# Twelve matmuls without a reader behind the last product of layer 0's MLP, ahead of layer 1's first keys

## The chip, the cores and the metric

The kernel runs on one core of one Trainium2 chip. The metric is the device time of one execution in microseconds (us); the number compared is the median of several executions. TensorE is called PE in the profile, its weight loads PEld, VectorE DVE, ScalarE ACT, GpSimd POOL, and SyncE, which here only issues DMAs, SP.

## The reference

Four layers run one after another on four images of 192 channels and 64 x 64 pixels, all in float32. Layer 0 is a deformable attention block that ends with an MLP; layer 1 is a full attention over the 4096 pixels of an image; layer 2 is attention in overlapping windows with a gated MLP; layer 3 is a depthwise convolution with computed weights. The change lies where layer 0 ends and layer 1 begins:

```python
# layer 0, its end
h1 = layer_norm(xs2, gamma2, beta2)
m = gelu(h1 @ w_fc1 + b_fc1) @ w_fc2 + b_fc2          # 192 -> 768 -> 192
x = xs2 + m
# layer 1
g_x = conv1x1(x, g_w, g_b);  theta_x = conv1x1(x, theta_w, theta_b);  phi_x = conv1x1(x, phi_w, phi_b)
f = softmax(einsum("bon,bom->bnm", theta_x, phi_x), axis=-1)          # 4096 x 4096
x = conv1x1(einsum("bnm,bom->bon", f, g_x), W_w, W_b) + x
```

## The kernel before, in words

The images are handled one by one, `b` from 0 to 3. For each image the stages follow each other so: layer 0's gather (its sampled pixels fetched by indirect DMAs into `ring`, L572, and weighted on ACT and DVE, L578 to L583), layer 0's MLP (`mlp0`), layer 1's keys and values (`keys`), layer 1's attention (`layer1`), layer 2's windows, and `rest`, which holds layer 2's MLP and layer 3. Work of the next image is laid beside that of the present one: the gather of image b+1 runs beside `layer1` of image b, and `mlp0` of image b+1 is a generator that `rest` of image b advances as it goes. Only image 0's `mlp0` runs alone. `offsets` of images 2 and 3, the convolution and the tables for the gather, is woven with `keys` of images 1 and 2. So beside `keys` of image 0 there are only the gather's first fetches, and beside `keys` of image 3 there is nothing.

The program is written through a tile framework. It places waits by the data that an instruction reads and writes, and it may order instructions of one engine otherwise than the text has them, by its own plan of times; within an engine the resulting order is fixed.

`mlp0` works on 8 chunks of 512 pixels (`NCH` is 8, `CN` is 512). The 192 channels are laid out as 128 rows and a second piece of 64. For a chunk, `widen` makes the 768 hidden channels (L796, L803) and applies Gelu on ACT (L809) into `gl`; `narrow(1)` (L821) and `narrow(0)` (L818) multiply by the second weight into a PSUM tile `p`, and one DVE instruction (L825) adds bias and input and writes the result over `x`. Then three DMAs on SP (L844) write the chunk to `x_flat`, in HBM.

`keys` reads the same image back, in 8 chunks of 512 pixels: a DMA on SP (L855) into a tile `xk` with two buffers, two products with `phiT` (L858, tile `tp`), an ACT copy with bias into `ph` (L859), eight small products with `gT` (L863, tile `g`), and a DVE copy into `gx` (L866). `layer1` then loads pieces `xc` of the image (L899), makes `th` from them (L902), and multiplies it with `ph` into scores `s` (L910).

`ident` (a 128 x 128 identity) and `bias` (layer 2's relative position bias, 128 rows of 384 numbers) are constants in SBUF that live from the first gather to the end.

One `nc.tensor.matmul` of float32 in the text appears as two MATMUL records in the trace: the two products at L858 of one chunk are four records.

## Time and profile before

| what | value |
|---|---|
| median of 3 runs | 6941.55 us (6940.37 to 6947.27) |
| the profiled execution's own time | 7023.62 us |
| its span | 7021.7 us |
| mean granted TensorE clock | 0.925 of full |
| PE busy | 6255.7 us, 89% of the span |
| DVE, ACT, POOL busy | 4813.5, 3724.2, 2070.0 us |
| PE's wait for `xk` at L858, by tile | 69.1 us with its weight loads, 11 times |

The profile comes from one execution with the profiler on. Its time is 82 us above the median of the others, so differences are made against its own span and carried over to the median. The views used are the page (busy times, the span in 40 slices, the costliest groups), the timeline (instructions in order, with the idle time before them and what ended it), busy time by stretches with the granted clock, one line's or one tile's instructions, and the chain of waits, which follows the work that ended last back in time. In the timeline a row is: start, duration of the merged group, engine, line, operation, output<-inputs, shape, count, and in brackets the idle time of the engine before it with what ended it.

### The profile page before, as it was taken

What the parts mean: (1) busy time and instruction counts of PE and PEld (TensorE: products, weight loads), DVE (VectorE), ACT (ScalarE), POOL (GpSimd) and SP (SyncE); (2) the same over time, 40 slices, a digit from 0 to 9 for tenths busy, and PEclk for the clock granted to TensorE, in tenths of its full rate; (3) what the DMA queues carried; (4) which work ended last, traced back from release to release, by engine and by line L of the source; (5) the groups of instructions that cost most, each with busy time, mean ns of one, the idle gap of its engine ahead of it and who ended that gap; (6) DMA issues with size and microseconds to landing.
All of it is one profiled execution on the core that took longest, in us unless ns stands there. A gap on an engine that the chain in (4) does not pass through costs nothing.

```text
span 7021.7 us, 114826 instructions
## 1 busy us (share of the span) xinstructions
PE 6255.7 (89%) x45020; PEld 4235.4 (60%) x45020; DVE 4813.5 (69%) x7087; ACT 3724.2 (53%) x6214; POOL 2070.0 (29%) x2265
## 2 busy tenths in 40 slices
PE   7677999998988899998988889999998889989976
PEld 3445578885643468886644458887554457766532
DVE  3654269984677759995586849996577757755656
ACT  3654368874544358884544348885444335535331
POOL 2654047761200037772200016773210000012100
PEclk8878989998999899998999999999999979989998
DMA  7885246761010177762010066773110010010000
GB/s 233 261 308 177 75 141 215 219 195 38 15 34 14 57 223 219 224 209 75 11 42 14 24 214 198 225 217 111 28 30 20 16 49 12 12 36 12 4 7 20
DMA packets 363195, 743.42 MB, mean 106 GB/s; under 512 B 52647, under 2 KB 246871, under 8 KB 361886
## 3 DMA queue, kind: packets, MB, share of 16 engines
q0 software_dynamic: 95040, 467.22, 20.9%
q1 hardware_dynamic: 267614, 268.87, 12.9%
q8 instruction: 355, 5.82, 0.4%
q14 instruction: 186, 1.52, 0.1%
HBM read 628.06 MB, written 106.21 MB: 105 GB/s over the span
## 4 chain that ended last, share of the span: by engine, by line
PE 65%; DVE 17%; ACT 7%; DMA 4%; issue 4%; another core or an unknown queue 1%; SPq 1%; POOL 1%; ACTq 0%; DVEq 0%; POOLq 0%
PE s L910 12%; PE y L976 11%; PE h L590 7%; PE v L1136 2%; PE qk L1061 2%; DVE ha L1304 2%; PE qk L1062 2%; PE h L1504 2%; DVE ga L1304 2%; PE po L482 1%; DMA ring<-table,idx 1%; PE t L1144 1%; DVE gate L1304 1%; PE zm L1515 1%; PE tp L858 1%
## 5 line engine op out<-in xcount | busy, mean ns | idle before, releaser
L572 POOL DMA_INDIRECT ring<-table,idx x1188 | 1677.8, 1412 | 1155.1 <-DVE row L579 281.1
L910 PE MATMUL s<-ths,ph 96*128 96x256 f32 x4096 | 985.6, 387 | 7.8 <-ACT ths L904 4.1
L910 PEld LDWEIGHTS s<-ths,ph 96*128 96x128 f32 x4096 | 788.3, 194 | 147.6 <-ACT ths L904 13.9
L578 ACT ACTIVATE row<-ring,pos 128x384 f32<-128x384 f32 x1188 | 697.6, 609 | 235.7 <-DVE xo L583 152.5
L579 DVE SCALAR_TENSOR_TENSOR row<-ring,fr,row 128x384 f32<-128x384 f32 x1188 | 698.9, 612 | 96.1 <-ACT row L578 73.2
L976 PE MATMUL y<-sc,gx 128*97 128x256 f32 x3008 | 723.5, 379 | 0.0
L582 ACT ACTIVATE xo<-row,pos 128x192 f32<-128x192 f32 x1188 | 505.7, 449 | 156.8 <-remote 60.4
L976 PEld LDWEIGHTS y<-sc,gx 128*97 128x97 f32 x3008 | 490.3, 164 | 122.4 <-issue 1.1
L583 DVE SCALAR_TENSOR_TENSOR xo<-row,fr,xo 128x192 f32<-128x192 f32 x1188 | 464.9, 411 | 117.4 <-ACT xo L582 64.8
L590 PE MATMUL h<-ti,xo 128*128 128x192 f32 x2376 | 465.1, 330 | 5.7 <-DVE xo L583 5.7
L912 ACT COPY sc<-s 128x1024 f32<-128x1024 f32 x376 | 377.0, 1003 | 170.6 <-PE s L910 162.2
L973 DVE TENSOR_TENSOR sc<-sc,mbs 128x1024 f32<-128x1024 f32 x376 | 448.6, 1217 | 15.0 <-ACT mbs L936 14.2
L917 DVE TENSOR_TENSOR top<-top,sc 128x1024 f32<-128x1024 f32 x282 | 344.3, 1221 | 130.8 <-ACT sc L912 119.9
L590 PEld LDWEIGHTS h<-ti,xo 128*128 128x128 f32 x2376 | 406.2, 191 | 42.6 <-DVE xo L583 10.7
L974 ACT ACTIVATE sc<-sc 128x1024 f32<-128x1024 f32 x376 | 393.2, 1054 | 27.7 <-DVE sc L973 19.2
L1120 DVE TENSOR_REDUCE es<-ex 128x6 f32<-128x384 f32 x264 | 133.2, 546 | 379.2 <-ACT ex L1116 379.2
L590 PE MATMUL h<-kept,xo 128*128 128x192 f32 x990 | 257.9, 396 | 120.5 <-DVE xo L583 59.7
L1545 POOL COPY gate<-gate 128x192 f32<-128x192 f32 x12 | 4.2, 348 | 1109.9 <-ACT gate L1538 1109.9
L590 PEld LDWEIGHTS h<-kept,xo 128*128 128x128 f32 x990 | 185.4, 221 | 207.7 <-DVE xo L583 95.9
L1304 DVE SCALAR_TENSOR_TENSOR ga<-gate,v,ga 128x1024 f32<-128x1024 f32 x234 | 299.7, 1281 | 7.2
L976 PE MATMUL y<-se,gx 128*97 128x256 f32 x1088 | 259.3, 379 | 0.5 <-ACT yn L982 0.5
L1509 ACT ACTIVATE z<-h,bias_fc1T 128x512 f32<-128x512 f32 x192 | 117.8, 686 | 232.8 <-PE h L1506 232.4
(383 smaller groups left out, 11530.6 us busy)
## 6 DMA issues: line engine op xcount, KB each, us to landing
ti<-table SPq DMA_DIRECT2D x396, 96.0 KB
table<-tt SPq DMA_DIRECT2D x24, 1056.0 KB
ring<-table,idx POOLq DMA_INDIRECT x1188
xnd<-xn SPq DMA_DIRECT2D x4, 3270.0 KB
table<-kept SPq DMA_DIRECT2D x12, 1056.0 KB
table<-tt SPq DMA_DIRECT2D x44, 288.0 KB
xi<-in_x_dram SPq DMA_DIRECT2D x32, 384.0 KB
xk<-xd SPq DMA_DIRECT2D x32, 384.0 KB
```

The lines of the kernel that those rows point to most:

```text
L572: nc.gpsimd.indirect_dma_start(out=gt.rearrange("p r q c -> p (r q c)"), out_offset=None, in_=table[:, :], in_offset=bass.IndirectOffsetOn ...
L578: nc.scalar.activation(row, gt[:, :, 0, :], AF.Copy, scale=pos[:, t, 9 + tap : 10 + tap])
L579: nc.vector.scalar_tensor_tensor(row, gt[:, :, 1, :], fr[:, t, 9 + tap : 10 + tap], row, ALU.mult, ALU.add)
L582: nc.scalar.activation(xo[:, j, :], row[:, 0, :], AF.Copy, scale=pos[:, t, tap : tap + 1])
L583: nc.vector.scalar_tensor_tensor(xo[:, j, :], row[:, 1, :], fr[:, t, tap : tap + 1], xo[:, j, :], ALU.mult, ALU.add)
L590: nc.tensor.matmul(acc[m // 2][:, bass.ts(m % 2, C)], lhsT=xo.rearrange("p j c -> p (j c)")[:, bass.ts(m, 128)], rhs=tt, start=t == 0 and ...
L910: nc.tensor.matmul(p[:, t, :], lhsT=ph[:, bass.ts(G * g + t, 128)], rhs=ths[i], start=True, stop=True)
L912: nc.scalar.copy(to, p)
L973: nc.vector.tensor_tensor(ex, ex, mbs[i].unsqueeze(1).to_broadcast([128, G, QN]), ALU.add)
L974: nc.scalar.activation(ex, ex, AF.Exp)
L976: nc.tensor.matmul(py, lhsT=gx[:, G * g + t, :], rhs=ex[:, t, :], start=g == 0 and t == 0, stop=g == NG - 1 and t == G - 1,)
L1304: nc.vector.scalar_tensor_tensor(acc[:, b], src(tap, b), w[:, tap : tap + 1], acc[:, b], ALU.mult, ALU.add)
```

## The change

Behind the last chunk's `narrow(0)` in `mlp0`, after the DMAs of its result were issued, `keep_warm` adds 12 products of `ident` with `bias`, each over 384 columns, into the PSUM tile `p` that `narrow(0)` returned. Each starts a new sum, and nothing reads `p` afterwards. `mlp0` is called once for each image, so 48 products are added in all. Nothing is taken away.

```diff
+    def keep_warm(p, n):
+
+        columns = bias.rearrange("p e h j -> p (e h j)")
+        for _ in range(n):
+            nc.tensor.matmul(p[:, 0:384], lhsT=ident, rhs=columns, start=True, stop=True)
+
     def mlp0(b, m2, pool, sb, ps):
...
                 nc.vector.scalar_tensor_tensor(to, p, VW["l0_bfc2"][:, k], to, ALU.add, ALU.add)
+                return p
...
             hn = norm(i + 1)
-            narrow(0)
+            p = narrow(0)
             for of, to in parts(x, HN, x_flat[b % 2], CN * i):
                 nc.sync.dma_start(out=to, in_=of)
+            if i == NCH - 1:
+                keep_warm(p, 12)
```

## The prediction

> **What bounds the kernel now.** I read the page first, then the rows of L858, then the timeline and the stretches around each start of the keys.

> ```profile
> span 7021.7 us, 114826 instructions
> PE 6255.7 (89%) x45020; PEld 4235.4 (60%) x45020; DVE 4813.5 (69%) x7087; ACT 3724.2 (53%) x6214; POOL 2070.0 (29%) x2265
> L858 PE MATMUL tp<-xk,phiT x128: 592/1061/1169, 858.1 to 5741.0; 96*96 96x512 f32 x128
> L863 PE MATMUL g<-gT,xk x512: 246/420/422, 861.6 to 5745.0; 96*128 96x96 f32 x171
> ```

> PE is busy 89% of the span, so its pace matters. The rows of the keys (minimum, median, maximum in ns) show medians nearly twice the minima: most of them run at half speed. The timeline of PE for image 3 shows where:

> ```profile
> 5677.65 5.42 PE L818 MATMUL o<-gl,fc 128*128 128x512 f32 x12
> 5683.42 0.74 DVE L825 SCALAR_TENSOR_TENSOR xa<-o,wide,xa 128x512 f32<-128x512 f32 x1
> 5690.88 3.73 PE L858 MATMUL tp<-xk,phiT 96*96 96x512 f32 x4 [7.81 <-DMA xk<-xd]
> 5694.40 3.57 PE L863 MATMUL g<-gT,xk 96*128 96x96 f32 x16
> 5697.76 3.62 PE L858 MATMUL tp<-xk,phiT 96*96 96x512 f32 x4
> ```

> After the MLP's last product PE waits 7.81 us for the first keys. Then eight chunks follow without a gap, 6.77 us apart, to 5745.0. The granted clock (the column after PE, PEld, DVE, ACT and POOL) in stretches of 4 us:

> ```profile
> 5680.00:5684.00 4.00, 3.07 (x8) 1.04 (x6) 4.00 (x7) 0.00 (x0) 0.16 (x1) 1.00 0.19 47
> 5684.00:5688.00 4.00, 0.00 (x0) 0.00 (x0) 4.00 (x7) 0.00 (x0) 0.00 (x0) 0.78 0.90 289
> 5692.00:5696.00 4.00, 4.00 (x12) 2.35 (x11) 0.00 (x0) 0.68 (x1) 0.00 (x0) 0.50 0.72 195
> 5740.00:5744.00 4.00, 4.00 (x14) 2.81 (x13) 0.00 (x0) 0.68 (x1) 0.00 (x0) 0.50 0.08 29
> 5752.00:5756.00 4.00, 4.00 (x14) 3.30 (x13) 0.20 (x1) 1.49 (x2) 0.00 (x0) 0.69 0.00 0
> ```

> The clock falls to 0.5 in the wait (0.78 over 4 us puts the fall at 5686.2) and stays there through the whole keys stage, though PE is busy all the time; it returns at 5754.5, in the scores. Image 0 is the same from 856.3 to 921. In images 1 and 2 the wait is 9.17 and 9.28 us and the clock returns 11 to 13 us after the first keys. The chain of waits runs through `tp` and `g` in these stages, so their pace is paid for.

> [...] the clock's changes lie on a grid of 3.413 us. [...] laying the matmul records over that grid (a record's columns at the rate below), windows of 0.83 to 0.92 filled in image 3's keys never raised the clock, while windows of `tp` and `pm_l` back to back (1.00) did; a full clock was lost in windows filled under about 0.4 to 0.48, and in none over 0.5. [...] the four gaps here are 5.8 to 9.3 us, and all four lose the clock.

> **The new matmuls.** 12 products are 24 records of 384 columns. The 12 records of L818 take 0.43 us apiece for 512 columns at full clock, so 0.32 for 384; the same width at L1061 starts every 0.33. 24 x 0.33 = 7.9 us at full clock for each image. They write the tile that L825 reads, so they start when L825 ends, about 1.1 us after the last product, with the clock still full [...]. Nothing but the keys is queued behind them on PE. They read constants, and no DMA or other engine waits for them, so the transfer of `xk` (SP, issued behind the result's write) stays as it is.

> - Image 3: L825 ends 5684.16, the new work ends 5692.1, keys were ready at 5690.88: 1.2 us late.
> - Image 1: 2424.0 to 2431.9, keys ready 2432.07: hidden. Image 2: 4047.1 to 4055.0, ready 4055.29: hidden.
> - Image 0: 853.05 to 861.0, ready 858.05: 2.9 us late.

> **What the clock is worth.** The warm pace is in image 1:

> ```profile
> 2455.88 1.92 PE L863 MATMUL g<-gT,xk 96*128 96x96 f32 x16
> 2464.42 1.88 PE L858 MATMUL tp<-xk,phiT 96*96 96x512 f32 x4
> 2456.00:2460.00 4.00, 4.00 (x37) 2.61 (x36) 1.30 (x3) 2.00 (x3) 0.00 (x0) 1.00 0.49 119
> ```

> From start to start a warm `tp` is 1.72 us and a warm `g` 1.76: a chunk is 3.48 instead of 6.77. It fills its windows (4 x 0.43 + 16 x 0.08) / 3.48 = 0.86, above what loses a clock; image 1 keeps 1.00 through such a mix from 2444 on. So I take it as kept.

> *Image 3.* The second chunk's load is issued at 5691.37 and its packets end at about 5696, so a hole of some 0.9 us follows the first chunk. Later loads take about 3 us from the release of their buffer, less than the 3.48 of the chunk between. Keys end at 5692.1 + 0.9 + 8 x 3.48 = 5720.8 instead of 5745.0: 24 us. `th` gains 0.8 and the scores from 5747.65 to 5754.5, now at full clock, 3.4. **28 us.**

> *Images 1 and 2.* Cold are `tp`, `g`, `tp` and most of `pm_l`: 1.7 + 1.6 + 1.7 + 0.6 = 5.6 us. The loads of the next chunk and of `xi` land by about 2436; I give 0.6 to such holes. **5 us each**; behind it PE is the chain, so it stays.

> *Image 0.* The first two chunks are warm, 861.0 to 868.0, and `th` takes 0.5. Then the third is late: eleven gathers fill the DMA engines from 857 to 876, and its load, issued when the first chunk is done, took 8.3 us:

> ```profile
> 873.61 3.70 PE L858 MATMUL tp<-xk,phiT 96*96 96x512 f32 x4 [0.84 <-DMA xk<-xd]
> ```

> The first chunk ends at 864.5 instead of 865.17, so the load lands at about 872.8: a hole of 4.3 us, which on any phase of the grid leaves a window under 0.4 filled. The clock is lost and six chunks stay cold. **1 us.**

> Sum: 28 + 5 + 5 + 1 = 39 us of 7021.7. The profiled execution is 82 us above the median; these stages have no reason to differ, so 6941.55 - 39 = 6902.5, taken as 6902. What isn't shown in the trace is that a new matmul starts right behind L825: at best at once, at worst some us later if planned behind other work; image 3 and 0 pay each us, images 1 and 2 after 0.2.

> **Rivals.**

> 1. *Image 0 stays warm too.* [...] six chunks save 3.3 us each and the scores 2: 22 more, 6880. [...] Against: the eleven gathers. 0.15.
> 2. *The clock is not held by the keys.* Then only the first window or so is warm: 3 us each in images 1 and 2, 2 in image 3, -3 in image 0: about 5 us, 6937, within 0.2%, which is about what a measurement of this kernel can tell from no change. Against: the 1.00 in image 1. 0.09, with lesser shifts of the plan.
> 3. *The first load waits for the new matmuls*, as a buffer's release can if it is counted on PE: the price is the issue's delay, from 853.5 to 861 (and then behind the gathers: 11), 2428.6 to 2431.9 (3.4), 4051.8 to 4055 (3.2), 5686.3 to 5692.1 (5.8): 24 us slower, 6965, with the clock lost again. It decides if the first L855 carries a wait on PE. Against: the new work touches no SBUF tile that is written. 0.06.
> 4. *The matmuls land elsewhere*, in PE's order behind the keys' wait: 4 x 7.9 = 32 us of pure work, 6973. Against: they are ready 4 to 8 us before the keys. 0.03.

> **How the numbers follow.** The forecast has 0.67, rival 1 0.15, 2 0.09, 3 0.06, 4 0.03. Faster by over 0.2% (14 us): 0.82 less 0.01 for a planner's shift that eats it, 0.81; within: 0.10; slower: 0.09. The forecast's own range is 6890 to 6916: image 3 at 22 to 30, images 1 and 2 at 3 to 6. The range reaches to rival 1 with some more and to the middle of rival 2: 6874 to 6940.

> **What would show it.** In the profile after: PE's wait at L858 down from 69.1 us to under 25; clock 1.00 through image 3's keys, chunks 3.5 us apart; the scores of image 3 some 28 us earlier against its last MLP product; a hole of 3 to 5 us after image 0's second chunk with 0.5 behind it; 96 new records, each near 0.33. Wrong is the forecast if image 3's chunks start warm and fall back, or if the first L855 is issued later after L825 than the 2.2 us of image 3 before.

## The result, and the profile after

The change makes the kernel faster by about 25 us: 6915.61 us (median of 10 runs, 6884.62 to 6935.18) against 6940.96 before (10 runs, 6921.96 to 6977.93). The ratio is 0.9952, with a 95% interval of 0.9932 to 0.9973. A second comparison gave 6908.4 (20 runs) against 6938.35 (43 runs), ratio 0.9961 (0.9945 to 0.9976). The forecast was 6902, from 39 us of gain. Its mechanism is in the trace, part by part; the size of the gain is too large, and the experiments say why.

The page after, its span and busy times (PE, PEld, DVE, ACT, POOL; share of the span; number of instructions):

```profile
span 6926.8 us, 115018 instructions
PE 6241.2 (90%) x45116; PEld 4215.2 (61%) x45116; DVE 4818.3 (70%) x7087; ACT 3732.5 (54%) x6214; POOL 2088.4 (30%) x2265
```

PE executes 96 instructions more and is busy 14.5 us less. The span fell by 95 us, far more than the median. Some 57 us of that are not the change's: in the profiled execution of before, image 0's `mlp0` ended at 853.05 us, after at 795.79, and nothing of the change has run by then. Three repeats of the kernel before (below) ended it at 799.4 to 799.7, so the one profiled first was the odd one. Its delay built up in layer 0's gather of image 0: the last fetch (L572) was issued at 625.0 us there and at 570.9 to 571.3 in the three repeats. Why that gather was slower stays open. All comparisons below are therefore made from the end of the DVE instruction that finishes `mlp0` of an image (L825 before, L831 after).

The change moves line numbers: L858, L863 and L855 are now L867, L872 and L864, and the new products are L692. Everything that touches the tile `xk` in the trace after (minimum, median and maximum duration in ns, first and last start; then what PE's idle time before it ended on, in us and times):

```profile
L872 PE MATMUL g<-gT,xk x512: 246/275/421, 805.4 to 5652.9; 96*128 96x96 f32 x171
L867 PE MATMUL tp<-xk,phiT x128: 590/592/1137, 803.7 to 5650.8; 96*96 96x512 f32 x128
...
  DMA xk<-xd: 10.3, 9
```

The median `tp` record is down from 1061 to 592 ns: most keys now run at full clock. The wait for the load is 10.3 us where it was 69.1. The new records:

```profile
L692 PE MATMUL o<-bias,ident x96: 486/486/590, 795.8 to 5622.8; 128*128 128x384 f32 x96
```

Each lasts 0.49 us, but they overlap in PE. The timeline of PE in image 3 has the 24 of one image as one row (start, duration, and in brackets the idle time before it and its releaser):

```profile
5615.31 8.01 PE L692 MATMUL o<-bias,ident 128*128 128x384 f32 x24 [1.15 <-DVE xa L831]
5623.16 1.88 PE L867 MATMUL tp<-xk,phiT 96*96 96x512 f32 x4
5624.88 1.92 PE L872 MATMUL g<-gT,xk 96*128 96x96 f32 x16
5627.43 1.93 PE L867 MATMUL tp<-xk,phiT 96*96 96x512 f32 x4 [0.63 <-DMA xk<-xd]
...
5649.47 1.93 PE L867 MATMUL tp<-xk,phiT 96*96 96x512 f32 x4 [0.26 <-DMA xk<-xd]
5651.24 1.92 PE L872 MATMUL g<-gT,xk 96*128 96x96 f32 x16
```

They take 8.01 us, so one starts every 0.33. They begin 1.15 us after the last product, the first keys follow without a pause, and the chunks run 3.5 to 4.3 us apart to the end, 3.76 on average, with holes of 0.63 and 0.26 us. The stretches of 4 us over the same image, with busy time of PE, PEld, DVE, ACT and POOL and then the granted clock:

```profile
5616.00:5620.00 4.00, 4.00 (x14) 2.35 (x13) 4.00 (x8) 0.00 (x0) 0.00 (x0) 1.00 0.84 287
5624.00:5628.00 4.00, 3.37 (x21) 2.44 (x20) 0.56 (x1) 0.68 (x1) 0.00 (x0) 1.00 0.57 156
5648.00:5652.00 4.00, 3.75 (x23) 2.57 (x22) 0.56 (x1) 0.74 (x2) 0.00 (x0) 1.00 0.23 70
```

1.00 throughout, where before had 0.50 from the wait to the scores.

Image 0 is the part that did not gain. Its timeline, and two of its stretches:

```profile
795.85 8.01 PE L692 MATMUL o<-bias,ident 128*128 128x384 f32 x24 [0.85 <-DVE xa L831]
803.69 1.88 PE L867 MATMUL tp<-xk,phiT 96*96 96x512 f32 x4
...
816.54 3.70 PE L867 MATMUL tp<-xk,phiT 96*96 96x512 f32 x4 [5.30 <-DMA xk<-xd]
820.03 3.57 PE L872 MATMUL g<-gT,xk 96*128 96x96 f32 x16
```

```profile
808.00:812.00 4.00, 3.24 (x21) 2.28 (x19) 0.56 (x1) 0.68 (x1) 2.96 (x4) 1.00 1.05 334
812.00:816.00 4.00, 0.00 (x0) 0.00 (x0) 0.00 (x0) 0.00 (x0) 0.83 (x1) 0.58 1.03 328
```

Two chunks are warm, then PE waits 5.30 us for the third chunk's load beside full DMA engines (share 1.03), loses the clock, and the other six chunks are cold. In image 1 the keys are warm from the first one, but a hole opens before the second chunk:

```profile
2369.76 1.96 PE L867 MATMUL tp<-xk,phiT 96*96 96x512 f32 x4
2371.56 1.92 PE L872 MATMUL g<-gT,xk 96*128 96x96 f32 x16
2375.00 2.77 PE L867 MATMUL tp<-xk,phiT 96*96 96x512 f32 x4 [1.52 <-DMA xk<-xd]
```

That hole costs the clock for one window of the grid, 2375.95 to 2379.36, which is why the `tp` behind it takes 2.77 us. The grid stands in the trace's records of the granted clock: they have two values, 0.50 and 1.00, and the 203 changes in the first profile of before and the 189 in that of the change lie on multiples of 3.413 us from the first of them, to within 2 ns.

To compare images, I take the time from the end of `mlp0` to the end of the 64th record of the scores `s`, which takes in the keys, `th` and the first scores. In us, in the two profiled executions and in the runs of the experiments:

| kernel | image 0 | image 1 | image 2 | image 3 |
|---|---|---|---|---|
| before, profiled first | 79.6 | 144.7 | 142.7 | 80.9 |
| before, repeat 1 | 64.2 | 143.4 | 142.2 | 56.2 |
| before, repeat 2 | 78.6 | 141.7 | 142.8 | 68.5 |
| before, repeat 3 | 78.8 | 141.4 | 142.8 | 74.8 |
| change | 79.7 | 140.0 | 138.0 | 53.4 |
| change, repeat | 79.8 | 138.9 | 136.9 | 53.7 |
| 4 products for 12 | 59.2 | 143.6 | 142.3 | 54.3 |
| products in image 3 alone | 64.7 | 142.2 | 143.9 | 53.2 |
| products on a 32 x 32 corner | 84.5 | 147.7 | 147.8 | 86.1 |
| image 0's hole filled | 58.5 | 137.7 | 141.4 | 53.6 |
| four `xk` buffers in image 0 | 51.9 | 139.9 | 137.5 | 53.6 |
| four buffers, no products | 79.3 | 142.5 | 143.3 | 57.4 |
| four buffers, 8, 12, 12, 10 products | 50.3 | 139.4 | 142.2 | 76.7 |
| four buffers, 8, 12, 12, 12 products | 49.2 | 139.1 | 139.5 | 53.3 |

Between the first two profiles the gains are 0, 4.7, 4.6 and 27.5 us by image, 37 in all. Over all rows, image 3 took 53.2 to 53.7 us in the six profiles with its 12 products on the full array, and 56.2 to 80.9 in the five without products. Image 1 took 137.7 to 140.0 with them and 141.4 to 144.7 without (six profiles each). Image 2 gains less surely: 136.9 to 142.2 with, 142.2 to 143.9 without. Of those six profiles with products, image 1 lost the clock in the hole before its second chunk in five, image 2 in three, for one or two windows.

### The profile page after: what moved, and what is told of

It is laid out like the page before. It is cut to its first block, busy times and chain, and to the rows that moved or that the text cites. A ratio compares the mean times of both kernels' runs of the same rounds, so it can differ in the third digit from the quotient of the medians.

```text
span 6926.8 us, 115018 instructions
## 1 busy us (share of the span) xinstructions
PE 6241.2 (90%) x45116; PEld 4215.2 (61%) x45116; DVE 4818.3 (70%) x7087; ACT 3732.5 (54%) x6214; POOL 2088.4 (30%) x2265
## 3 DMA queue, kind: packets, MB, share of 16 engines
q14 instruction: 187, 1.52, 0.1%
## 4 chain that ended last, share of the span: by engine, by line
PE 63%; DVE 18%; ACT 7%; DMA 6%; issue 4%; POOL 1%; SPq 1%; DVEq 0%; ACTq 0%; POOLq 0%
PE s L919 11%; PE y L985 10%; PE h L590 6%; DMA ring<-table,idx 3%; PE v L1145 2%; PE qk L1070 2%; PE qk L1071 2%; DVE ha L1313 2%; PE h L1513 2%; DVE ga L1313 2%; PE h L802 1%; PE t L1153 1%; PE po L482 1%; DVE gate L1313 1%; PE zm L1524 1%
## 5 line engine op out<-in xcount | busy, mean ns | idle before, releaser
L572 POOL DMA_INDIRECT ring<-table,idx x1188 | 1691.3, 1424 | 1065.3 <-DVE row L579 245.0
L582 ACT ACTIVATE xo<-row,pos 128x192 f32<-128x192 f32 x1188 | 505.2, 448 | 68.5 <-DVE row L579 40.6
```

Source lines behind the costliest of these rows:

```text
L572: nc.gpsimd.indirect_dma_start(out=gt.rearrange("p r q c -> p (r q c)"), out_offset=None, in_=table[:, :], in_offset=bass.IndirectOffsetOn ...
L582: nc.scalar.activation(xo[:, j, :], row[:, 0, :], AF.Copy, scale=pos[:, t, tap : tap + 1])
```

## The experiments

**Theory:** the products keep PE at work through the wait, so the clock stays full and the keys hold it. **Rivals:** the gain comes from something else that the products shift; or any product holds the clock, whatever its size; or image 0 can't be kept warm even without its hole.

**Four products for twelve.**

```diff
-                keep_warm(p, 12)
+                keep_warm(p, 4)
```

> 4 products instead of 12: 8 records, 2.6 us, so PE then stands idle for over 5 us before the keys of images 1 to 3. Read from the end of L831 (the MLP's last DVE instruction) to the end of the 64th score record. Clock theory: a whole window of 3.413 us fits into what is left of the wait, the clock is lost as before, and image 3 takes 81 us (80.9 before, 53.4 with 12), images 1 and 2 within 2 us of 144.7 and 142.6. Rival, that work in the wait helps by its amount or by the order it brings: image 3 gains a third of the 27.5, about 72 us.

Measured: 6897.9 us, one run. In images 1 and 2, where the rest of the wait stays long, nothing is left of the gain (143.6 and 142.3). Images 0 and 3 nevertheless are quick. Image 0 kept the clock through its shorter wait (1.55 us), lost it at 819.4 in the hole behind the second chunk (5.46 us) and had it back at 833.0. The timeline of image 3:

```profile
5584.48 2.85 PE L692 MATMUL o<-bias,ident 128*128 128x384 f32 x8 [1.15 <-DVE xa L831]
5591.05 3.61 PE L867 MATMUL tp<-xk,phiT 96*96 96x512 f32 x4 [3.72 <-DMA xk<-xd]
5594.45 2.00 PE L872 MATMUL g<-gT,xk 96*128 96x96 f32 x16
```

The wait left over was 3.72 us; the expectation had worked it out too long. It did lose the clock, at 5591.2, but the clock was back at 5594.6: the first `tp` ran cold from 5591.05 to 5594.45, nearly the whole window of the 3.413 us grid from 5591.2 to 5594.6. So a stage that loses the clock can get it back by how its products lie on the grid. That became the next question.

**Products in image 3 alone.**

```diff
-            if i == NCH - 1:
+            if i == NCH - 1 and b == B - 1:
```

> The 12 products behind image 3's MLP alone. Clock theory: each image stands for itself, so image 3 takes 53 to 54 us from L831's end to the 64th score record (53.4 with all), images 0, 1 and 2 are as before: 79.6, 144.7 and 142.6. Rival, that the images' gains hang together through the plan or through later transfers: image 3 gains less than 25 us, or images 1 and 2 move too.

Measured: 6906.0 us, one run. Image 3 has its whole gain (53.2). Image 1 (142.2) lies within the repeats of before, image 2 (143.9) 1.1 us above them, so neither has a gain: image 3's does not hang on theirs. Image 0, without any products, took 64.7 and not 79: its clock came back in its keys, again at the end of a cold `tp` (830.85 to 834.26) that filled one window of the grid.

**The same columns on a corner of the array.** The products use 32 of the 128 rows and 32 of the 128 columns of `ident`.

```diff
-            nc.tensor.matmul(p[:, 0:384], lhsT=ident, rhs=columns, start=True, stop=True)
+            nc.tensor.matmul(p[0:32, 0:384], lhsT=ident[0:32, 0:32], rhs=columns[0:32], start=True, stop=True)
```

> The same 12 products for each image with 32 rows and 32 columns of the array instead of 128 by 128; as long in time, a sixteenth of the array. If the clock follows the time in which PE streams, nothing changes: image 3 takes 53 to 54 us from L831's end to the 64th score record and its clock stays at 1.00. If it follows the share of the array that works, the wait counts as idle: the clock falls during the new products, the last of them run at 0.65 us each, the keys start up to 4 us late, and image 3 takes 81 to 85 us.

Measured: 6969.3 us, one run, beside 6944.83 for the kernel before. Two rows of its timeline and two of its stretches, image 3:

```profile
5621.79 12.40 PE L692 MATMUL o<-bias,ident 32*32 32x384 f32 x24 [1.14 <-DVE xa L831]
5634.12 3.73 PE L867 MATMUL tp<-xk,phiT 96*96 96x512 f32 x4
```

```profile
5621.00:5625.00 4.00, 3.21 (x10) 1.08 (x11) 4.00 (x7) 0.00 (x0) 0.00 (x0) 1.00 0.83 251
5625.00:5629.00 4.00, 4.00 (x8) 1.15 (x7) 2.42 (x6) 0.00 (x0) 0.00 (x0) 0.51 0.57 184
```

PE is busy all the time (4.00 of 4.00), and the clock still falls at about 5625, at the end of the first window that this work filled (to 0.94 of its time). The new work then takes 12.4 us instead of 8.0, and the stage ends later than before (86.1). Time at work is not enough to hold the clock: these products don't hold it, where those of the keys, 96 x 96, do (1.00 through image 3's keys with the change, in windows filled to 0.65 to 0.86).

This run cuts rows and columns together. Other stages of the traces separate them. Three rows of PE in the first profile of before, with a stretch of each of the two stages:

```profile
89.27 11.81 PE L482 MATMUL po<-xn,wp 96*32 96x384 f32 x108
92.00:96.00 4.00, 4.00 (x42) 1.46 (x36) 0.00 (x0) 0.00 (x0) 0.00 (x0) 1.00 0.76 219
6941.27 3.78 PE L1580 MATMUL f<-z,fc2T 128*128 128x512 f32 x4 [1.38 <-DVE z L1568]
6946.43 1.98 PE L1580 MATMUL f<-z,fc2T 128*128 128x512 f32 x4 [1.38 <-DVE z L1568]
6944.00:6948.00 4.00, 2.62 (x6) 0.68 (x4) 2.34 (x2) 0.00 (x0) 0.00 (x0) 0.78 0.00 0
```

The products of L482 use 96 rows and 32 columns of the array (96*32 in the row), and hold the clock for 11.8 us (1.00). Those of L1580, over 128 rows, raise it at 6945.7 although their window was filled to only 0.74, a low case of the limit given below. So, as far as these stages show, the rows count and the columns don't: my reading is that what the corner lacks is its share of the rows, a quarter, and not of the array, a sixteenth.

In the fourteen profiles of the table, with the time that each record's streamed columns take (512 in a `tp`) laid over the grid as in the prediction, windows of 96-row products alone raised the clock from 0.985 of the time (9 of 804 windows at half clock lie on the wrong side) and lost it under 0.49 (1 of 1249 at full clock). Windows of 128-row products alone raised it from about 0.78 (35 of 1148) and lost it under 0.36 (31 of 5905). These limits are fitted to the windows counted. Rows (of 128) times time gives nearly the same two for both: 0.74 and 0.78 for the rise, 0.37 and 0.36 for the loss. The corner, 32 rows at 0.94 to 1.00, comes to 0.25 at most, under the second limit. Windows with other products, those of 64 rows among them, are not in these counts, and no run cuts the rows alone.

**Image 0's hole filled.** Eight more products, 96 columns of the array wide, behind the second chunk of image 0, in the `tp` tile that has been read.

```diff
+            if b == 0 and i == 1:
+                for _ in range(8):
+                    nc.tensor.matmul(
+                        warmed[:, 0:384], lhsT=ident[:, 0:P], rhs=bias.rearrange("p e h j -> p (e h j)"), start=True, stop=True
+                    )
```

> The change as it is, and 8 more products (16 records, 5.2 us, 96 of 128 columns of the array) behind the second chunk of image 0's keys, where PE waited 5.3 us for the third chunk's load. Clock theory: the clock stays, chunks 3 to 8 of image 0 take 3.5 to 4 us instead of 6.77, and from L831's end to the 64th score record image 0 takes 57 to 61 us instead of 79.7; images 1 to 3 as with the change. Rival, that behind the gathers the loads bind: the chunks stay further apart than 5 us and image 0 gains under 8 us.

Measured: 6905.88 us, one run. The hole of 5.30 us became 5.33 us of work and a rest of 0.71, the clock held (the four records of the next `tp` took 1.93 us), and image 0 took 58.5 instead of 79.7. So that one hole was what cost image 0 its gain. Image 2 was not as with the change (141.4): a hole before its second chunk cost it the clock from 3991.5 to 3998.3.

**The hole taken away.** Four buffers for `xk` in image 0, so that the third and fourth load are issued before the gathers' transfers fill the engines; once with the change, once without it.

```diff
-                    b, ph, gx, s2.enter_context(pool_of(name="l1k", bufs=2)),
+                    b, ph, gx, s2.enter_context(pool_of(name="l1k", bufs=4 if b == 0 else 2)),
```

> The change, and four buffers instead of two for xk in image 0, so that the third and fourth chunk's loads are issued before the gathers fill the DMA engines. Clock theory: no hole behind the second chunk, image 0's keys at full clock throughout, 51 to 55 us from L831's end to the 64th score record (79.7 with the change alone, 58.5 with the hole filled by products); images 1 to 3 as with the change. Timed: some 20 us below the change, 50 to 65 below before. Rival, that only the holes cost: image 0 gains the 5.3 us of the hole and no more, about 74 us.

> The kernel before with the four buffers alone, no new products. Clock theory: the clock is lost in the first wait, the keys run at half speed, and the earlier loads are worth the 0.8 us of the old hole: image 0 takes 77 to 80 us from L825's end to the 64th score record, unless one 3.41 us product of the keys falls on a window of the grid, which would bring the clock back in the middle of the stage (62 to 72). Rival, that the early loads are what counts for image 0: near 55 us.

> The change as it is, once more beside the others on one chip. Clock theory: image 3 53 to 54 us, images 1 and 2 138 to 140 from L831's end to the 64th score record; image 0 79 to 80 with the clock lost in its hole, or 57 to 66 if a window of the grid brings it back. Timed: 25 to 40 us below before.

Measured in one comparison, against 6938.35 for before: with the change 6900.75 us (14 runs, ratio 0.9951, 0.9934 to 0.9967), the change itself 6908.4 (0.9961, 0.9945 to 0.9976), the buffers alone 6934.94 in one run. The timeline of image 0, four buffers with the change:

```profile
795.26 8.01 PE L692 MATMUL o<-bias,ident 128*128 128x384 f32 x24 [0.84 <-DVE xa L831]
...
810.05 1.88 PE L867 MATMUL tp<-xk,phiT 96*96 96x512 f32 x4
...
820.96 1.93 PE L867 MATMUL tp<-xk,phiT 96*96 96x512 f32 x4 [0.31 <-DMA xk<-xd]
```

The third chunk follows at once, the longest hole is 0.31 us, and image 0 takes 51.9 instead of 79.7. Without the products the same buffers leave it at 79.3: early loads don't help keys that run cold. The saved 28 us of that one profile are only 8 in the medians (some 20 were expected, and 50 to 65 under before, where 38 were measured), and the intervals overlap; image 0 need not lose as much in every execution, as the last experiment shows for the kernel before.

**Fewer products.** On top of the four buffers, as many products as the wait of each image seemed to need.

```diff
-                keep_warm(p, 12)
+                keep_warm(p, (8, 12, 12, 10)[b])
```

> As with four buffers in image 0, and 8, 12, 12 and 10 products for images 0 to 3, as many as the wait holds. Clock theory: images 0 and 3 start their keys when they land, some 2.5 and 1.2 us earlier; image 0 takes 48 to 53 us and image 3 52 to 53 from L831's end to the 64th score record. Timed: 3 us below the one with 12 products each, which the runs may not tell apart. Rival, that the clock is lost where fewer products leave a rest of the wait: image 0 or 3 near 80.

Measured: 6921.36 us (14 runs, ratio 0.9977, 0.9957 to 0.9997), 20.6 us slower in the same comparison than with four buffers and 12 everywhere. Image 0 is as wished (50.3), image 3 is cold (76.7). Its timeline:

```profile
5582.57 6.72 PE L692 MATMUL o<-bias,ident 128*128 128x384 f32 x20 [1.15 <-DVE xa L831]
5589.12 1.88 PE L867 MATMUL tp<-xk,phiT 96*96 96x512 f32 x4
5590.84 1.92 PE L872 MATMUL g<-gT,xk 96*128 96x96 f32 x16
5594.59 2.21 PE L867 MATMUL tp<-xk,phiT 96*96 96x512 f32 x4 [1.83 <-DMA xk<-xd]
```

The first keys start 1.3 us earlier, but the second chunk's load is where it was: its hole grew from 0.63 to 1.83 us, the window from 5592.7 to 5596.1 was filled to 0.43, and the clock went. The last two products of image 3, which the forecast booked as 1.2 us lost, were covering the next load.

**Fewer products in image 0 alone, and the kernel before again.** The first tests that reading; the repeats ask how often the kernel before gets its clock back by itself.

```diff
-                keep_warm(p, (8, 12, 12, 10)[b])
+                keep_warm(p, (8, 12, 12, 12)[b])
```

> The change with four buffers for image 0's key chunks, and 8 products instead of 12 in image 0 alone (12 in the others). Theory (the products must reach to within about 1.5 us of the next load that the keys wait for; with four buffers image 0 has no such load, in image 3 the second chunk's load has): image 0 as with 10 to 8 products before, 50.3 us; image 3 warm again, 53 to 54 instead of 76.7; image 1 139 to 140 and image 2 137 to 143; time 6890 to 6905, about 20 us under the version that trimmed image 3 too, 2 under the one with 12 everywhere. Rival (image 3 was cold in the trimmed version by chance and not by the number of products): image 3 at 53 or 77 with no link to the number, time 6895 to 6925.

> The kernel before itself, once more, to see whether its clock in images 0 and 3 is the same in every execution. Theory of chance: behind the first keys' waits the clock is lost, and comes back inside the keys only where one of their 3.41 us products at half clock happens to cover one whole window of the 3.413 us grid. Then the 64th score record ends at 57 to 62 us from the end of the last addition where it came back, and at 79 to 83 where it did not, with little between, and over three executions of the kernel before at least one of the six stages (images 0 and 3) is of the first kind. Rival: the profile shown is what the kernel before always does: 79 to 82 us in all six. Images 1 and 2: 142 to 145 in both.

> As the first repeat of the kernel before: chance, image 0 and 3 each at 57 to 62 or 79 to 83 us, not the same in all repeats; rival, 79 to 82 in both. By chance at 3 in 6 (what the runs so far with such a stage gave) the mean over the repeats is near 70 us in each; by the rival near 80.

> As the first repeat of the kernel before: chance, image 0 and 3 each at 57 to 62 or 79 to 83 us, not the same in all repeats; rival, 79 to 82 in both.

Measured: the version with 8, 12, 12 and 12 products took 6890.3 us (7 runs, 6870.57 to 6908.58) against 6940.4 for before, ratio 0.9928 (0.9895 to 0.9961). Image 3 is warm again (53.3), image 0 keeps 49.2. It has the lowest median of all versions, 50 us under before; its lead over the change itself (0.9961) lies within the intervals. The trimmed 10 products in image 3 were profiled once, so that this number always loses the clock isn't shown; the 20.6 us above and the 31 us between the medians of the two trimmed versions, from two comparisons, fit it.

The repeats of before took 6918.26, 6929.21 and 6949.62 us. Image 3 ended at 56.2, 68.5 and 74.8, image 0 at 64.2, 78.6 and 78.8: not one case as in the rival, but not two as in the theory either. The timeline of image 3 in the second repeat shows the return in the sixth chunk:

```profile
5632.86 3.57 PE L863 MATMUL g<-gT,xk 96*128 96x96 f32 x16
5636.22 3.56 PE L858 MATMUL tp<-xk,phiT 96*96 96x512 f32 x4
5639.62 1.92 PE L863 MATMUL g<-gT,xk 96*128 96x96 f32 x16
```

and its stretches the clock:

```profile
5632.00:5636.00 4.00, 4.00 (x17) 3.47 (x16) 0.00 (x0) 0.68 (x1) 0.00 (x0) 0.50 0.08 22
5636.00:5640.00 4.00, 4.00 (x11) 1.79 (x10) 0.56 (x1) 0.18 (x1) 0.00 (x0) 0.55 0.32 98
5640.00:5644.00 4.00, 4.00 (x27) 2.96 (x27) 0.56 (x1) 1.19 (x2) 0.00 (x0) 1.00 0.29 85
```

The clock returned at 5639.6. The grid has a window from 5636.2 to 5639.6, and the `tp` of that chunk ran from 5636.22 to 5639.62. In the first repeat it was the second chunk (`tp` from 5614.86, window from 5615.0), in the third the eighth (`tp` from 5670.28, window from 5670.2). Windows of the keys before these, filled to 0.77 to 0.98 of their time, never raised the clock. A cold chunk takes 6.77 us and two windows 6.83, so a chunk slides by some 0.06 us against the grid: it depends on where the first keys begin whether a `tp` comes to cover a window early, late, or, as in the first profile (1.2 us off), never.

## Why the prediction was right, and what was off

- **The bound.** The clock lost in the wait, and not the wait itself, was the price: confirmed. After the change PE does 8 us more work in image 3 and ends the stage 27.5 us earlier.
- **The windows.** In image 3 the clock came back in chunk 2, 6 or 8 of the repeats, and in the first profile only in the scores: the `tp` with which it came back began within 0.14 us of a window's start, those of the first profile 1.0 to 1.3 us behind one. It came back where a window was filled far enough, from 0.985 of the time by products of 96 rows and from about 0.78 by products of 128; in the first profile 54 us of keys without a hole stayed at half clock, none of their windows filled to more than 0.92. Holes well under the four waits of 5.8 to 9.3 us lost it too: in the trimmed version one of 1.83 us in a loose mix, and in image 1 of the change one of 1.52.
- **The new matmuls.** 24 x 0.33 = 7.9 us forecast, 8.01 measured. Keys late by 1.2 us in image 3 (7.90 after `mlp0` against 6.72) and by 2.9 in image 0 (7.90 against 5.00), hidden in images 1 and 2: all as worked out. The loads' issue did not move (0.45 us after the end of `mlp0` in image 0, before and after).
- **Image 3.** 28 us forecast, 27.5 between the two profiles; the hole after the first chunk was 0.63 us for a forecast 0.9, and the chunks came 3.76 us apart on average, that hole included, for 3.48 without it.
- **Images 1 and 2.** 5 us each forecast, 4.7 and 4.6. Image 1 has a hole of 1.52 us where 0.6 was allowed, and lost the clock in it for a window. That the clock is kept once the wait is filled, as taken there, held in this profile for image 2 but not for image 1; that the size came out so near is in part luck, and against the average of four profiles of before image 1 gains 3.4.
- **Image 0.** 1 us forecast, 0 measured. The hole was 5.30 us for a forecast 4.3, with the clock lost behind it as said.
- **What was mis-sized.** The step "these stages have no reason to differ, so 6941.55 - 39" carried the profile's own 39 us over to the median. They do differ: the profile shown was an execution in which image 3 stayed cold to the end of its keys. Over the four executions of before in the table, image 3 takes 70.1 us on average, and the change's two 53.6: 16.5 us instead of 27.5. Image 0 takes 75.3 before and 79.7 after, -4.4 in these few executions; images 1 and 2 gain 3.4 and 5.1. The sum is 20.6, beside medians that differ by 25.4 and 30.0; so few profiles can't place the rest. Image 3 of the run with four buffers and no products (57.4) and image 0 of the run with products in image 3 alone (64.7), which had none either, were of the quick kind as well. The change makes image 3's best case the usual one, and part of that before had by luck.
- **"Filled" as time.** The reading of the windows by time alone was wrong as a rule for keeping the clock: on 32 rows of the array 0.94 of the time did not hold it, and as a rule for raising it: 0.98 was too little in the keys' 96 rows (image 0 of the first profile, the windows from 880.2 and 887.1 us), while 0.74 was enough in the 128 rows of L1580.
- **Rivals.** Image 0 warm (1) did not come in the two profiles of the change; it takes the hole's removal. The clock not held by the keys (2) and matmuls elsewhere in the order (4) are refuted by the rows above. For rival 3 the sign was badly chosen: image 0's first load does carry a wait on PE, in the kernel before as well, on an earlier product that is long done.

How often the kernel before gets the clock back, and how often the change does in image 0, is known from so few executions that it stays open as a rate.

## What to carry to other kernels

Price a wait of TensorE by what runs behind it as well as by its length: here a wait of 7.8 us cost 27 us in the keys that followed, in the first profile, and 8 us of products that nobody reads bought it back, as long as they reach near enough to the next load and use enough of the array: 32 rows of 128, on 32 columns, didn't do. Before pricing from one profile, ask whether its clock lies on the grid by chance, and profile the kernel before more than once: one execution gave 37 us where four gave 21. And look for the next hole: what held image 0 back was the third load, which two more buffers bring forward.
